# Causal attention stage on one Trainium2 core: rearranging q, k, x, maxima, denominators and outputs through DRAM images

## The chip, the core and the metric

The program runs on one core of a Trainium2 chip. A core has TensorE (PE in the profile; PEld is its weight loads), VectorE (DVE), ScalarE (ACT), GpSimd (POOL) and SyncE (SP), which here issues nearly all DMAs. The metric is the device time of one execution in microseconds (us); before the change the median of three runs is 1862.79 us (1861.15 to 1863.95).

## What is computed

The input is x of 4 batches x 1024 tokens x 256 features, all float32. Two parts follow each other: a causal attention with 16 heads of 16 features, then two layers of local attention and feed-forward. The change lies in the first part alone:

```python
def _L0_attn_ref(x, wq, bq, wk, bk, wv, bv, wo, bo):   # x is layernorm(x)
    q, k, v = proj(wq, bq), proj(wk, bk), proj(wv, bv)      # 16 heads of 16
    scores = jnp.einsum('bhqd,bhkd->bhqk', q, k) * scale
    mask = jnp.triu(jnp.full((t, t), NEG, jnp.float32), k=1)
    attn = jax.nn.softmax(scores + mask, axis=-1)
    out = jnp.einsum('bhqk,bhkd->bhqd', attn, v)
    out = out.transpose(0, 2, 1, 3).reshape(b, t, d)
    return out @ wo + bo

x = x + _L0_attn_ref(_layernorm(x), ...)
x = x + _L0_ffn_ref(_layernorm(x), ...)        # the two local layers
```

## The kernel before

**Chunks.** The causal stage works in 16 chunks n = 0 to 15, each one batch (n div 4) and four heads (n mod 4). A head has 16 features and takes a strip of 32 partitions, so that four heads fill the 128 partitions of a tile and TensorE multiplies the four side by side. `qbuf` and `kbuf` hold q and k of four chunks in turn (chunk n in buffer n mod 4). Row 16 of each strip carries the row maximum in q and -1 in k, so that the product of the turned scores already has the maximum taken off.

**Two passes over the scores.** In chunk n, TensorE makes the scores of chunk n+1 with queries in the partitions ("s", line 928). VectorE reduces them to row maxima (lines 936 and 938, into `nmax`). At the same time TensorE makes the scores of chunk n with keys in the partitions ("t", also line 928), ScalarE takes their exponentials (line 949, `et`), GpSimd zeroes what lies above the diagonal (line 955), and TensorE multiplies by the values (line 985, "av"). The value tile has a column of ones, so that row 16 of each output strip is the softmax's denominator. ScalarE copies each product out of PSUM and GpSimd adds it up (lines 1003 and 1004).

**Slots and the plan.** A chunk has 9 slots (`NU`). A slot u runs `pair(n, u, 0)`, `pair(n, u, 1)` (the s and t products of four heads), the value products of the slot before, and then whatever `plan[n][u]` lists. The plan is written by hand with `put(n, u, function)`, and a u of 9 or more falls into the next chunk. Nothing reorders it: every engine, and SP's queue of DMAs too, runs its instructions in the order in which the code emits them. Score products that need the second half of q (tokens 512 and on), or the maxima of the second half, begin in slot 2, in the second of its two groups.

**The jobs in the plan.**
- `norm`, `prep_x`, `turn_x` (lines 770, 783, 805): layer norm of the next batch, during the first two chunks of a batch (n mod 4 = 0 and 1). `turn_x` turns blocks of 32 x 32 on VectorE and issues 16 DMAs for each group of four token tiles, which put the blocks in their places in `xnT`.
- `project` (864): a quarter of the q or k projection for two chunks, 16 matmuls, into `dense`. `prep_b` (826): the values of two token tiles, 32 matmuls.
- `spread` (883): 16 rows of `dense` into each strip of `qbuf` and `kbuf`, 8 DMAs of 32 KB for one chunk's half.
- `put_maxima` (963), at slots 3 and 8 for the halves 0 and 1 of the next chunk: one turn on VectorE (`mt`), four DMAs to a DRAM tile `way`, and one DMA back into row 16 of the strips of `qbuf` (line 972), which waits for the four.
- `put_out` (1011) and `put_oT` (1022), for half 0 at slots 4 and 5 and for half 1 at slots 1 and 2 of the next chunk: VectorE turns the 128x512 sum (line 1014) and takes the reciprocal of the denominators (1016), GpSimd multiplies (1017), VectorE turns back (1026), and four DMAs move the 16 rows of each head into `oT` (1030).
- `out_b`, `out_s`, `out_c` (1035, 1054, 1068): output projection of two token tiles (32 matmuls), the sum with x, and its layer norm into `y_sb`. They run at slots 7 and 8 of a batch's last chunk and at 5 and 8 of the chunk after it.
- `swap_x` (1064) writes a batch's x to DRAM (`x_keep`) at slot 8 of chunks 6, 10 and 14; `load_x` brings a later batch in; `load_attn`, `load_tab` and `scale_tab` load and scale the weights and tables of the first local layer in chunks 2 to 5.

Of the kernel before, what the change touches and what calls it, by code (L numbers as in the profile page):

```python
# [51 lines left out]
def kernel_body(  # L52
# [621 lines left out]
    with actx:  # L674
        aw = actx.enter_context(tc.tile_pool(name="aw", bufs=1))
        a1 = actx.enter_context(tc.tile_pool(name="a1", bufs=1))
        a2 = actx.enter_context(tc.tile_pool(name="a2", bufs=2))
        a4 = actx.enter_context(tc.tile_pool(name="a4", bufs=4))
        a5 = actx.enter_context(tc.tile_pool(name="a5", bufs=5))
# [37 lines left out]

        nmax = aw.tile([P, 2, STRIP], F32, name="nmax")

        oT = aw.tile([P, 2, T], F32, name="oT")  # L720

        def clear():

            nc.vector.memset(qbuf[1], 0.0)
            nc.vector.memset(kbuf[1], -1.0)
            nc.vector.memset(qbuf[2], 0.0)
            for v in v_sb:
                nc.gpsimd.memset(v[:, :, H * VW :], 0.0)
                nc.gpsimd.memset(
                    v[:, :, 0 : H * VW].rearrange("p k (h s) -> p k h s", s=VW)[  # L730
                        :, :, :, ONE : ONE + 1
                    ],
                    1.0,
                )

        def clear_more():
            nc.gpsimd.memset(kbuf[2], -1.0)
            nc.gpsimd.memset(qbuf[3], 0.0)
            nc.gpsimd.memset(kbuf[3], -1.0)

# [17 lines left out]
        WARM = 26  # L758
        stats, xnTs, dense, avs_, mxs = {}, {}, {}, {}, {}
        qTs, kTs = (lambda n: qbuf[n % 4]), (lambda n: kbuf[n % 4])  # L760
# [43 lines left out]

        def turn_x(b, g, i):

            if i == 0:
                stats[b, "turn"] = b2.tile([P, GRP, 2, 4, 32], F32, tag="xturn", name=f"xturn_{b}_{g}")
            xturn = stats[b, "turn"]
            for t in (2 * i, 2 * i + 1):  # L810
                nc.vector.transpose(
                    xturn[:, t].rearrange("p c j r -> p (c j r)"), stats.pop((b, "xn", GRP * g + t))
                )
            if i == 0:
                return
            dst = xnTs[b][:, GRP * g : GRP * g + GRP].rearrange("p t c n -> p (t c) n")
            src = xturn.rearrange("p t c j r -> p (t c) j r")
            for d in range(4):
                for a in range(4):
                    j = (a + d) % 4  # L820
                    nc.sync.dma_start(  # L821
                        dst[32 * j : 32 * j + 32, :, 32 * a : 32 * a + 32],
                        src[32 * a : 32 * a + 32, :, j, :],
                    )

# [57 lines left out]
        def spread(n, h, kq=nc.sync):  # L883

            b, c = divmod(n, NC4)
            ts = slice(h * 512, (h + 1) * 512)
            for which, dst in enumerate((qTs(n), kTs(n))):
                for j in range(4):
                    r = (c % 2) * 64 + j * HD
                    (kq if which else nc.sync).dma_start(  # L890
                        dst[STRIP * j : STRIP * j + HD, ts],
                        dense[b, c // 2, which][r : r + HD, ts],
                    )

        def pair(n, u, pr):
# [67 lines left out]
        def put_maxima(n, qb):  # L963

            mt = a2.tile([P, STRIP], F32, tag="mt", name=f"mt_{n}_{qb}")
            nc.vector.transpose(mt, nmax[:, qb, :])
            way = keep4.tile([4 * GRP, P], F32, tag="way", name=f"way_{n}_{qb}")
            for a in range(4):
                nc.sync.dma_start(
                    way[:, 32 * a : 32 * a + 32], mt[32 * a : 32 * a + 4 * GRP, :]  # L970
                )
            nc.sync.dma_start(
                qTs(n)[ONE:P:STRIP, qb * 512 : (qb + 1) * 512],
                way.rearrange("(j i) x -> j (i x)", j=4),
            )

        def products(n, u):
# [14 lines left out]
            if kt == 0:  # L992
                avs_[n, "acc"] = a2.tile([P, 512], F32, tag="avs", name=f"avs_{n}_{qb}")
                (nc.vector.tensor_copy if n == NCH - 1 else nc.scalar.copy)(avs_[n, "acc"], av)
# [16 lines left out]
        def put_out(n, qb):  # L1011
# [7 lines left out]
            )  # L1019
            avs_[n, "t1", qb] = t1  # L1020

        def put_oT(n, qb):
# [68 lines left out]
        def quarters(n, b, d, first, *slots):  # L1091
            for i, u in enumerate(slots):
                put(n, u, project, b, d, (first + i) % 2, (first + i) // 2)

        for n in range(NCH):
            b, c = divmod(n, NC4)
            more = b + 1 < B
            if n >= 1:
                put(n, 1, put_out, n - 1, 1)
                put(n, 2, put_oT, n - 1, 1)  # L1100
            put(n, 4, put_out, n, 0)
            put(n, 5, put_oT, n, 0)
            if c == 0:
                if b:
                    quarters(n, b, 1, 3, 0, 1, 3, 4, 6)
                    outs(n, 5, b - 1, 2)
                    put(n, 8, out_b, b - 1, 3)
                    put(n, NU + 6, out_s, b - 1, 3)
                    put(n, NU + 7, out_c, b - 1, 3)
                    put(n, 1, spread, n + 2, 0)  # L1110
                    put(n, 2, spread, n + 3, 0)
                else:
                    quarters(n, b, 1, 2, 0, 1, 2, 3, 4, 6)
                    put(n, 2, spread, n + 2, 0)
                    put(n, 3, spread, n + 3, 0)
                put(n, 7, spread, n + 2, 1)
                put(n, NU, spread, n + 3, 1)
            if c == 0 and more:
                for i, u in enumerate((0, 3, NU, NU + 3)):
                    put(n, u, norm, b + 1, 2 * i, 2 * i + 2)  # L1120
                for i, u in enumerate((4, 5, NU + 2, NU + 5)):
                    put(n, u, prep_x, b + 1, i)
                for i, u in enumerate((7, 8, NU + 7, NU + 8)):
                    put(n, u, turn_x, b + 1, i // 2, i % 2)
                n += 1
                quarters(n, b + 1, 0, 0, 4, 5, 7, 8)
                n += 1
                quarters(n, b + 1, 0, 4, 2, 3, 4, 5)
                for i in range(2):
                    put(n, i, spread, n + 2 + i, 0)  # L1130
                    put(n, 5 + i, spread, n + 2 + i, 1)
                for i in range(4):
                    put(n, (0, 1, 7, 9)[i], prep_b, b + 1, i)
                n += 1
                quarters(n, b + 1, 1, 0, 2, 3, 5)
                n -= 3
            if c == 3:
                outs(n, 7, b, 0)
                outs(n, 8, b, 1)
        n = -1  # L1140
        plan[n][0] = [(spread, (0, 1, nc.scalar)), (spread, (1, 0)), (spread, (1, 1))]
        put(n, 3, bias)
        put(n, 2, load_x, 1, 0, NW)
        for i, u in enumerate((4, 5, 6, 7)):
            put(n, u, prep_b, 0, i)
        put(n, 5, clear_more)
        quarters(n, 0, 1, 0, 7, 8)
        put(n, 7, load_x, 2, 0, NW)

        for n in range(-1, NCH - 1):  # L1150
            for half, u in enumerate((3, 8)):
                plan[n][u].insert(0, (put_maxima, (n + 1, half)))
        for b in range(B - 1):
# [233 lines left out]
```

## Time and profile before

| | us |
|---|---|
| median of three runs (lowest, highest) | 1862.79 (1861.15, 1863.95) |
| the profiled execution's own time | 1867.73 |
| its span, first to last instruction | 1866.0 |
| TensorE busy in the span | 1797.8 (96%) |
| VectorE, ScalarE, GpSimd busy | 1349.4, 1022.9, 1131.4 |
| mean granted TensorE clock | 0.974 |
| first exponential of chunk 0, last of chunk 15 | 57.5, 644.1 |
| the 16 chunks, shortest and longest | 28.8, 45.8 |
| SP's issue of one `spread` DMA, of one `turn_x` DMA | 0.59, 0.61 |

How to read it: busy time is the time in which an engine has an instruction in work. The ends of matmuls are modelled, so a busy TensorE may still be waiting a little. The granted clock is the share of TensorE's full speed that the chip allowed. A timeline row gives start, duration, engine, line, operation, `out<-in`, and in brackets the idle time before it with what ended it. "SPq" is SP's own queue: a row there is the issue of DMAs, not their transfer. In a list of waits, a row says who waited for whom, then the us in total, the number of times and the longest.

### The profile page before, as it was taken

What the parts mean: (1) busy time and instruction counts of PE and PEld (TensorE: products, weight loads), DVE (VectorE), ACT (ScalarE), POOL (GpSimd) and SP (SyncE); (2) the same over time, 40 slices, a digit from 0 to 9 for tenths busy, and PEclk for the clock granted to TensorE, in tenths of its full rate; (3) what the DMA queues carried; (4) which work ended last, traced back from release to release, by engine and by line L of the source; (5) the groups of instructions that cost most, each with busy time, mean ns of one, the idle gap of its engine ahead of it and who ended that gap; (6) DMA issues with size and microseconds to landing.
All of it is one profiled execution on the core that took longest, in us unless ns stands there. A gap on an engine that the chain in (4) does not pass through costs nothing.

```text
span 1866.0 us, 46190 instructions
## 1 busy us (share of the span) xinstructions
PE 1797.8 (96%) x16922; PEld 1055.2 (57%) x16922; DVE 1349.4 (72%) x4115; ACT 1022.9 (55%) x2558; POOL 1131.4 (61%) x1359
## 2 busy tenths in 40 slices
PE   8999998998999979889999999999999999999999
PEld 5444444554454345556656656666566656566576
DVE  5886886896889556667868768768667778678642
ACT  1665765775777635444555465554545555555621
POOL 3463584674475476667666666666667577586611
PEclk7998998998999989899999999999999999999999
DMA  3122111211110120455465565655656556555520
GB/s 109 39 34 80 33 34 37 64 34 36 57 27 15 33 74 7 68 98 98 82 105 88 103 102 90 140 95 96 119 121 121 104 100 117 108 106 111 96 51 23
DMA packets 785248, 142.52 MB, mean 76 GB/s; under 512 B 753552, under 2 KB 776064, under 8 KB 784512
## 3 DMA queue, kind: packets, MB, share of 16 engines
q1 hardware_dynamic: 784704, 139.25, 38.4%
q8 instruction: 135, 2.21, 0.5%
q14 instruction: 89, 0.73, 0.1%
q10 hardware_dynamic: 320, 0.33, 0.1%
HBM read 21.25 MB, written 8.65 MB: 16 GB/s over the span
## 4 chain that ended last, share of the span: by engine, by line
PE 84%; DVE 4%; SPq 4%; DMA 2%; POOL 2%; issue 1%; ACT 1%; DVEq 0%; ACTq 0%; POOLq 0%
PE pag L597 16%; PE pf L621 9%; PE t L928 7%; PE pw L507 6%; PE s L928 6%; PE av L985 6%; PE pq L228 5%; PE pk L228 5%; PE pv L228 5%; PE plo L465 5%; PE ls L386 4%; PE pp L765 3%; SPq L327 2%; SPq L821 2%; PE pr L765 1%
## 5 line engine op out<-in xcount | busy, mean ns | idle before, releaser
L949 ACT ACTIVATE et<-t 128x512 f32<-128x512 f32 x558 | 293.4, 602 | 88.4 <-PE s L928 59.0
L928 PE MATMUL t<-qbuf,kbuf 32*128 32x512 f32 (+1 forms) x1488 | 313.5, 513 | 3.2 <-DMA qbuf<-way 3.0
L597 PE MATMUL pag<-hnT,w 128*128 128x512 f32 x704 | 312.3, 593 | 0.8 <-DVE hnT L581 0.8
L928 PE MATMUL s<-kbuf,qbuf 16*128 16x512 f32 (+3 forms) x1440 | 305.3, 516 | 0.8 <-DVE nmax L938 0.8
L418 ACT ACTIVATE e<-e,lnmx 128x192 f32<-128x192 f32 (+2 forms) x512 | 224.0, 439 | 43.5 <-DVE lnmx L411 43.0
L432 POOL TENSOR_SCALAR e<-e,lrsum 128x192 f32<-128x192 f32 (+2 forms) x504 | 202.3, 422 | 21.1 <-DVE lrsum L429 15.6
L597 PEld LDWEIGHTS pag<-hnT,w 128*128 128x128 f32 x704 | 131.7, 190 | 142.4 <-issue 134.2
L928 PEld LDWEIGHTS t<-qbuf,kbuf 32*128 32x128 f32 x1488 | 149.8, 186 | 99.9 <-ACT et L949 37.1
L267 POOL TENSOR_TENSOR rn<-ss,mhalf 128x16 f32<-128x16 f32 x64 | 188.0, 2938 | 5.3
L1004 POOL TENSOR_TENSOR avs<-avs,part 128x512 f32<-128x512 f32 (+2 forms) x105 | 117.1, 1115 | 108.0 <-ACT part L1003 107.7
L264 POOL TENSOR_TENSOR rot<-rot,m 128x1024 f32<-128x1024 f32 x64 | 151.4, 2365 | 50.8 <-DVE m L245 42.8
L621 PE MATMUL pf<-w,act 128*128 128x256 f32 x768 | 173.1, 379 | 0.0
L938 DVE CUSTOM_DVE_ANT_0 s<-s,mask_c,mx 128x512 f32<-128x512 f32 (+1 forms) x240 | 132.7, 619 | 53.8 <-PE s L928 35.2
L928 PEld LDWEIGHTS s<-kbuf,qbuf 16*128 16x128 f32 x1440 | 146.6, 186 | 39.1 <-DVE nmax L938 11.4
L621 PEld LDWEIGHTS pf<-w,act 128*128 128x128 f32 x768 | 145.8, 190 | 26.6 <-issue 7.2
L611 DVE SCALAR_TENSOR_TENSOR act<-pag,cols_sb,ge 128x512 f32<-128x512 f32 x80 | 59.4, 742 | 139.4 <-ACT ge L610 95.0
L985 PE MATMUL av<-et,v_sb 128*32 128x512 f32 (+3 forms) x1536 | 158.5, 501 | 0.8 <-POOL et L955 0.4
L936 DVE TENSOR_REDUCE mx<-s 128x1 f32<-128x512 f32 (+1 forms) x240 | 133.9, 615 | 14.3 <-PE s L928 14.2
L266 POOL TENSOR_SCALAR ss<-ss 128x16 f32<-128x16 f32 x64 | 16.3, 254 | 197.7 <-DVE ss L261 195.6
L411 DVE CUSTOM_DVE_ANT_0 e<-ls,mask_h 128x192 f32<-128x192 f32 x408 | 116.7, 349 | 20.7 <-PE ls L386 20.7
L955 POOL TENSOR_SCALAR_AFFINE_SELECT et<-et 128x256 f32<-128x256 f32 x256 | 98.1, 407 | 54.9 <-ACT et L949 53.5
L507 PE MATMUL pw<-wlo,loT 128*128 128x256 f32 x512 | 129.0, 396 | 0.7 <-ACT loT L498 0.7
(268 smaller groups left out, 3595.0 us busy)
## 6 DMA issues: line engine op xcount, KB each, us to landing
ring_sb<-turned SPq DMA_DIRECT2D x880, 96.0 KB
qbuf<-dense SPq DMA_DIRECT2D x128, 32.0 KB
x_keep<-x SPq DMA_DIRECT2D x4, 1024.0 KB
xr<-x_keep SPq DMA_DIRECT2D x8, 512.0 KB
out_dram<-y_sb SPq DMA_DIRECT2D x16, 256.0 KB
oT<-t SPq DMA_DIRECT2D x126, 32.0 KB
kbuf<-dense SPq DMA_DIRECT2D x120, 32.0 KB
x<-in_x_dram SPq DMA_DIRECT2D x3, 1024.0 KB
```

Source lines behind the costliest of these rows:

```text
L228: nc.tensor.matmul(pq[i], lhsT=lhs[c], rhs=wt[:, c, i * INNER : (i + 1) * INNER], start=(c == 0), stop=(c == 1),)
L264: nc.gpsimd.tensor_tensor(rot, rot, m3, ALU.add)
L267: nc.gpsimd.tensor_tensor(rn[:, :, 0], ss, mhalf, ALU.pow)
L418: nc.scalar.activation(e[:, i, lo:nk], e[:, i, lo:nk], AF.Exp, bias=nmx[:, h : h + 1], scale=-1.0, accum_out=sums[:, h : h + 1],)
L432: by.tensor_scalar(e[:, i, lo:nk], e[:, i, lo:nk], rsum[:, h : h + 1], 1.0, ALU.mult, ALU.mult)
L507: nc.tensor.matmul(pw[:, 0:D], lhsT=oT[:, c, :], rhs=wt[:, c, :], start=(c == 0), stop=(c == 3))
L597: nc.tensor.matmul(pg[half], lhsT=wt[:, c, ff * P : (ff + 1) * P], rhs=hnT[:, c, :], start=(c == 0), stop=(c == 1),)
L621: nc.tensor.matmul(pf[:, 0:D], lhsT=act[:, f, i * P : (i + 1) * P], rhs=wt[:, f, :], start=(f == 0), stop=(f == NF - 1),)
L928: nc.tensor.matmul(o, lhsT=lhsT, rhs=rhs, start=True, stop=True)
L936: nc.vector.tensor_reduce(mxs[n + 1, i][:, h : h + 1], src, AX.X, ALU.max)
L949: nc.scalar.activation(et[:, h % 2, :], ts[h], AF.Exp, scale=ASCALE)
L985: nc.tensor.matmul(av[32 * j : 32 * j + 32, c0:512], lhsT=v_sb[b % 2][:, kt, VW * (4 * c + j) : VW * (4 * c + j) + STRIP], rhs=ets[j // 2] ...
```

## The change

- **DRAM images for q and k.** `img` holds two pairs of DRAM tiles of 256 x 1024, one for q and one for k, already in strips of 32 rows. `put_dense` writes a half of `dense` (128 rows) into the 16 used rows of eight strips, with one DMA each for q and k; `fetch` reads the 128 rows of one chunk's half with one DMA each. The unused rows are filled once by 16 DMAs (`clear_images`). `spread` is left for chunks 0 and 1.
- **Turned x.** `turn_x` writes its blocks to a DRAM tile with one DMA for each two token tiles; `fetch_x` reads a group of four back with four DMAs in rows of 32 values (128 bytes).
- **Maxima.** `put_maxima` writes the whole turned tile with one DMA; `get_maxima`, a slot later, reads it into row 16.
- **Outputs of chunks 0 to 13.** VectorE turns nothing. The denominator rows go out to DRAM (`den_out`), come in as 128 x 16 (`den_in`), VectorE takes the reciprocal and they go out again (`rec_out`), come back spread over each strip's 32 partitions with four DMAs (`rec_in`), and GpSimd multiplies 128x512 by 128x512 (`divide`). The product is written to DRAM, and for each two chunks one DMA (`get_oT`) gathers a half into `oT`. Chunks 14 and 15 keep `put_out` and `put_oT`.
- **The plan.** Projections of the next batch go to slots 4, 5, 6, 8 of the third chunk and 3, 5, 7 of the fourth (they stood at 2, 3, 4, 5 and 2, 3, 5). `out_b` moves from the last two slots of a batch and slots 5 and 8 of the next chunk to slots 5 and 7 of the next chunk and 1 and 2 of the one after, with `out_s` and `out_c` behind each.

The core of the diff:

```diff
+        img = [[keep.tile([2 * P, T], F32, name=f"img{i}{which}") for which in range(2)] for i in range(2)]
+        def clear_images(i):
+            for which, src in enumerate((qbuf[3], kbuf[3])):
+                dst = img[i][which].rearrange("(k r) (x t) -> k r x t", r=STRIP, t=256)
+                for x in range(4):
+                    nc.sync.dma_start(dst[:, HD:STRIP, x], src[:, 0:256])
...
+            nc.sync.dma_start(
+                stats[b, "way"][:, o : o + 4], xturn.rearrange("p t c j r -> p (t c) j r")
+            )
+        def fetch_x(b, g):
-            for d in range(4):
-                for a in range(4):
-                    j = (a + d) % 4
-                    nc.sync.dma_start(
-                        dst[32 * j : 32 * j + 32, :, 32 * a : 32 * a + 32],
-                        src[32 * a : 32 * a + 32, :, j, :],
-                    )
+            for j in range(4):
+                nc.sync.dma_start(
+                    dst[32 * j : 32 * j + 32].rearrange("q k (a r) -> q k a r", a=4),
+                    way[:, :, j, :].rearrange("(a q) k r -> q k a r", a=4),
+                )
...
+        def put_dense(b, d, h):
+                rows_ = img[(NC4 // 2 * b + d) % 2][which].rearrange("(k r) t -> k r t", r=STRIP)
+                nc.sync.dma_start(rows_[:, 0:HD, ts], dense[b, d, which][:, ts])
+        def fetch(n, h):
+            for which, dst in enumerate((qTs(n), kTs(n))):
+                nc.sync.dma_start(dst[:, ts], img[(n // 2) % 2][which][c * P : (c + 1) * P, ts])
...
+        def rec_out(n, qb):
+            nc.vector.reciprocal(rec, avs_.pop((n, "d1", qb)))
+            way = keep4.tile([4, 512], F32, tag="recway", name=f"recway_{n}_{qb}")
+            nc.sync.dma_start(way.rearrange("j (k x) -> (j k) x", x=16), rec)
...
+        def divide(n, qb):
+            nc.gpsimd.tensor_tensor(
+                t3, avs_.pop((n, "out", qb)), avs_.pop((n, "t1", qb)), ALU.mult
+            )
...
+                put(n, 0, get_maxima, n, 1)
+                    for u, fn in ((1, den_out), (2, den_in), (3, rec_out), (4, rec_in), (6, divide)):
+                        put(n, u, fn, n - 1, 1)
+                put(n, 4, get_maxima, n + 1, 0)
+                for u, fn in ((5, den_out), (6, den_in), (7, rec_out), (8, rec_in), (NU + 1, divide)):
+                    put(n, u, fn, n, 0)
...
-                quarters(n, b + 1, 0, 4, 2, 3, 4, 5)
+                quarters(n, b + 1, 0, 4, 4, 5, 6, 8)
+                put(n, 0, put_dense, b + 1, 0, 0)
+                put(n, 3, fetch, n + 2, 0)
+                put(n, 4, fetch, n + 3, 0)
+                put(n, NU, put_dense, b + 1, 0, 1)
+                put(n, NU + 1, fetch, n + 2, 1)
+                put(n, NU + 2, fetch, n + 3, 1)
...
+                    for i, u in enumerate((NU + 5, NU + 7, 2 * NU + 1, 2 * NU + 2)):
+                        outs(n, u, b, i)
```

## The prediction

> **What bounds the kernel now.** I read the page first. TensorE (PE) is busy 96% of the span, so time can only be won where PE stands idle, runs at a lower clock, or is fed too slowly. The change touches only the causal stage, whose last exponential ends at 644 us.
>
> ```profile
> PE 1797.8 (96%) x16922; PEld 1055.2 (57%) x16922; DVE 1349.4 (72%) x4115; ACT 1022.9 (55%) x2558; POOL 1131.4 (61%) x1359
> ```
>
> Second, a table of windows, one for each of the stage's 16 chunks (cut where the first exponential of a chunk, L949, starts). Columns: length, then busy time of PE, PEld, DVE, ACT and POOL, then the granted PE clock, DMA share, GB/s. Chunks 5, 6, 7 and 13:
>
> ```profile
> 247.90:284.10 36.20, 35.57 (x356) 17.38 (x352) 32.65 (x107) 25.30 (x50) 29.27 (x37) 1.00 0.18 31
> 284.10:329.90 45.80, 40.03 (x452) 18.72 (x448) 28.38 (x88) 26.79 (x56) 18.95 (x30) 0.89 0.22 41
> 329.90:365.90 36.00, 35.98 (x436) 18.28 (x435) 29.29 (x94) 26.36 (x53) 19.16 (x29) 1.00 0.21 71
> 555.40:585.50 30.10, 30.10 (x292) 15.11 (x290) 28.95 (x93) 23.28 (x45) 17.45 (x26) 1.00 0.09 20
> ```
>
> Chunk 6 takes 45.8 us where its neighbours take 36, with PE idle for 5.8 and the clock at 0.89; chunks 2 and 10 (45.2, 44.7) look the same. Third, PE's waits, then for chunk 2 SP's timeline, then two short windows, name the cause:
>
> ```profile
> PE pp L765 <- DMA xnT<-xturn: 10.3, 2, 5.7
> PE t L928 <- DMA qbuf<-way: 3.0, 4, 1.6
> ```
> ```profile
> 129.71 11.35 SPq L821 DMA_DIRECT2D xnT<-xturn  x16
> 141.16 2.46 SPq L890 DMA_DIRECT2D qbuf<-dense  x4
> ```
> ```profile
> 141.80:151.80 10.00, 9.03 (x60) 3.41 (x64) 3.04 (x9) 3.45 (x7) 0.73 (x1) 0.50 0.25 52
> 182.80:186.00 3.20, 3.20 (x32) 1.45 (x27) 2.52 (x9) 1.62 (x4) 2.31 (x5) 0.50 0.37 129
> ```
>
> SP needs 11.4 us merely to issue 16 transfers of turned x. PE waits 4.5 us for the last of them (5.75 in chunk 6, 4.4 in chunk 10) and then runs 10 us at clock 0.50. In chunk 3 a wait of 1.57 us for the maxima (L972) ends at 181.06, and some 3.4 us at 0.50 follow. SP's issuing, and the clock that a wait costs, are the prize. The second limit is VectorE: 29.0 of 30.1 us in chunk 13.
>
> **Prices.** PE's work in a chunk without project, prep_b and out_b: chunk 7 is 36.0 less three projections (0.87 each, the spacing of the four at 10.5 to 13.1 us), one prep_b and two out_b (1.9 each, the row of 32 matmuls at 362.83), 27.7; chunk 12 is 35.9 less five and two, 27.8. I use 27.9. A wait with its clock: chunks 2, 6, 10 should take 27.9 + 4 x 0.87 + 3 x 1.9 = 37.1, and chunk 2 takes 8.1 more for a wait of 4.5, so I put 8.5 on a wait of 4.5 us; chunk 3 takes 38.9 - 36.0 = 2.9 more for 1.57, so 3.5 for 2 us, 5 for 3. Waits of 0.6 us (chunk 11) cost no clock.
>
> **What goes.**
> - Turned x takes 2 + 4 transfers a group instead of 16, and its first user moves from slot 2 to slot 4: chunks 2, 6, 10 go from 135.7 to 3 x 37.1, -24.4.
> - VectorE loses two turns of 0.70 us for each half of chunks 0 to 13, 2.8 us a chunk, and the waits of up to 3 us that the second turn has for the transfers before it:
>
> ```profile
> DVE t L1026 <- DMA oT<-t: 5.5, 2, 3.0
> ```
>
> - Chunks 1, 5, 9 hold four projections only (27.9 + 3.5 = 31.4 us of PE) but take 36.9, 36.2 and 35.8, with VectorE busy 32: here its relief is worth time. And two out_b a batch move from chunks 3, 7, 11 to 5, 9, 13. With no new wait: chunk 1 31.4 (-5.5); 5 and 9 35.2 (-1.6 together); 3, 7, 11 32.4 (-14.1); 13 31.7 (+1.6); 4, 8, 12 36.05 (-1.2); 14 -0.7.
>
> Together **-46**; if VectorE is not what stretches chunks 1, 5 and 9, about -31. Cost nothing: the memsets taken from VectorE and GpSimd, and the 16 image-clearing issues (8 us of SP) beside chunks -1 and 0; get_maxima behind the first eight has four slots of cover.
>
> **What comes: SP's queue ahead of slot 2.** The maxima of half 1 are turned by VectorE (mt) just as a chunk begins. Slot 2 of that chunk needs them, and half 1 of the next chunk's q, 7.3 us later (chunk 7: mt at 329.74, second group of slot 2 at 337.02). Today they land after 5.4:
>
> ```profile
> 330.32 1.91 SPq L969 DMA_DIRECT2D way<-mt  x4
> 333.35 0.54 SPq L972 DMA_DIRECT2D qbuf<-way  x1
> 334.00 0.37 SPq L1066 DMA_DIRECT2D x_keep<-x  x1
> ```
>
> In the new order get_maxima stands behind all that slot 8 plans, and small transfers also wait for the bytes issued before them: in chunk 3 the four 2 KB writes behind the 1.5 MB weight load landed 5.2 us after the last issue, not 1.1 as here. I walk the queue from mt with 0.5 us an issue (L969 takes 0.46, large loads 0.35 to 0.58), 1.1 us to the first byte, and for 256 KB in 2 KB rows 0.8 us (the weights, 320 GB/s) to 1.5 us (the tables' 1 KB rows, 172 GB/s).
> - Chunks 7, 11: maxima out, get_oT, four rec_in, **x_keep (1 MB, 3.1 us at 320 GB/s), which now stands ahead**, two put_dense, get_maxima, then fetch, which waits until put_dense has landed. q lands 11.0 to 12.9 us after mt: a wait of 3.7 to 5.6. I take 4.5, 8.5 with its clock: +17. Chunk 3, without x_keep, waits 0.6 to 2.5, taken as 2: +3.5.
> - Chunk 1: four rec_in, four reads of turned x (4096 pieces of 128 B; the old transfers show 32.6% of 16 queues x 11.1 us over 4352 packets, 13.3 ns each, so 3.4 us), two fetches, get_maxima: landed at about 9.3, wait 2, +3.5. Chunks 5 and 9 now have an out_b ahead of slot 2: wait 1 each, +2. Chunks 2, 6, 10 have two prep_b there: 0.5 each, +1.5.
> - Chunk 15 reaches slot 2's second group 4.8 us after mt; x_keep and four output issues now stand in front: wait 3, +5.
>
> **GpSimd.** The divide is 128x512, 1.27 us (the row of L1004) for 0.62 (L1017), +18 us in all, but its 61 us of waiting for the reciprocal go, and two slots lie between rec_in and divide. What costs is the move of two out_b: their adds and out_c now meet prep_x and scale_tab (2.4 each) in chunk 5, where POOL is busy 29.3 already. The masks of slots 1 and 2, which the value products need, come 2 to 4 us late: +3. VectorE's reciprocal waits for den_in, issued one slot before; behind it stand the score evictions, and so PE. The path (POOL's sum, two landings of 2 us) leaves some 1.5 us: nothing, but about 1 us a chunk if that cover is gone.
>
> New costs: 17 + 3.5 + 3.5 + 2 + 1.5 + 5 + 3 = 35.5 (12 at the lower ends without clock, 55 at the upper with it). **Net -11**: the span of 1866.0 becomes 1855. The profiled run took 1867.7, the median is 1862.8; the same 11 off the median is **1852**.
>
> **Two rules that bear on it.** Half clock after 1.57 us of idling stands in the trace. The Trainium skill ("TensorE: Matmul & The Clock Gate", Part 1) has the clock fall only after a whole idle window of about 3.4 us; by it the waits of 2 and 3 us would cost no clock, and the sum would be an estimated 5 us better. No transfer here has an outermost count of eight. The skill ("DMA: Bandwidth & Descriptors", on why a DMA increments its semaphore by 16) spreads a DMA over the largest number up to 16 that divides the outermost counts of both sides, so put_dense and get_oT would get 8 of the 16 engines; by an estimate from that page, the sum would be 6 us worse.
>
> **Rivals.**
> - *Forecast, 45%*: **1852**, between 1838 and 1866.
> - *The queue hides it, 22%*: transfers run at 320 GB/s, waits stay under a microsecond outside chunks 7, 11 and 15, new costs 12: -34, **1829**. For it: chunk 7 has 1.9 us of cover today. Against: x_keep's new place.
> - *Slower, 25%*: the small reads. Turned x is now read from DRAM in pieces of 128 B, which no row shows. At 20 ns a piece instead of 13.3 the four reads take 1.7 us longer, directly ahead of q and the maxima in chunks 1, 2, 5, 6, 9, 10; waits of 2 to 4 us with their clock then cost 4 more each, +24: **1876**. From about 16 ns on the 11 us are used up.
> - *It doesn't do what it says, 8%*: x of the second group still lands after slot 4, and chunks 2, 6, 10 keep most of their wait: 1863.
>
> **Numbers.** 0.2%, 3.7 us, is about what a measurement of this kernel can tell from no change. Of the forecast's 45, 36 are faster, 5 the same, 4 slower; the second case is faster, the third slower, the fourth the same: faster 0.58, same 0.13, slower 0.29. The range takes in the second and third case with a little around them: 1826 to 1878.
>
> **What would show it.** Right: chunks 2, 6, 10 near 37 us with no wait for xnT; PE waits on qbuf<-way or qbuf<-img at slot 2 of chunks 7, 11, 15 with clock 0.50 after each; POOL over 33 us in chunk 5. Wrong: chunks 1, 5, 9 still at 36 with VectorE below 30 (then something else paced them); slot 2 without waits; or VectorE waiting for its reciprocals in every chunk.

## The result, and the profile after

The changed kernel is slower: 1878.4 us median of 4 runs (1877.4 to 1879.7) where the kernel before took 1863.4 in the same session (1861.2 to 1864.3). The ratio is 1.0083, with a 95% interval of 1.0065 to 1.0100. The forecast was 1852.

| profiled execution | before | after |
|---|---|---|
| its own time, span (us) | 1867.7, 1866.0 | 1878.5, 1876.7 |
| causal stage, first to last exponential | 57.5 to 644.1 | 54.6 to 669.1 |
| everything behind it | 1221.9 | 1207.6 |
| PE idle in the stage; periods at clock 0.50 there | 20.0; 4, 34 us in all | 32.0; 10, 71 us in all |

The stage became 28 us longer. It began 2.9 us sooner (so it did in a second profile of the kernel before), and the part behind it, whose code is the same, became 14.3 us shorter: the span shows only 10.7 of the 28.

The page of after. The instruction counts fell on VectorE (4115 to 4058), but PE, with the same 16922 matmuls, is busy longer:

```profile
span 1876.7 us, 45891 instructions
PE 1801.9 (96%) x16922; PEld 1056.2 (56%) x16922; DVE 1323.3 (71%) x4058; ACT 1023.1 (55%) x2558; POOL 1146.9 (61%) x1358
```

The table of windows of after, chunks 5, 6, 7 and 13, with the columns of the prediction:

```profile
245.40:290.80 45.40, 44.02 (x424) 22.72 (x426) 40.87 (x118) 27.06 (x51) 41.79 (x50) 0.92 0.37 95
290.80:333.50 42.70, 39.13 (x452) 19.23 (x451) 25.85 (x85) 26.75 (x56) 20.12 (x29) 0.92 0.33 84
333.50:372.60 39.10, 35.55 (x368) 16.70 (x362) 24.61 (x80) 25.14 (x51) 16.68 (x27) 0.91 0.40 131
570.20:605.90 35.70, 35.30 (x358) 17.95 (x355) 30.43 (x100) 24.44 (x48) 30.35 (x42) 1.00 0.27 84
```

Chunk 6 was to fall from 45.8 to 37 and stands at 42.7, with its clock still at 0.92. Chunk 5, which had run at 36.2 with its clock at 1.00, takes 45.4: GpSimd (the last busy time) went from 29.3 to 41.8 of it, VectorE from 32.7 to 40.9.

What PE waited for in the stage, and one wait of VectorE (us in all, times, longest). Waits for xnT are gone. Those for the maxima grew from 3.0 to 26.1:

```profile
DVE rec L1066 <- DMA d<-den: 26.6, 17, 3.1
PE t L953 <- DMA qbuf<-way: 26.1, 8, 4.7
...
PE s L953 <- DVE nmax L963: 3.1, 3, 1.4
...
PE s L953 <- DMA qbuf<-img: 1.8, 3, 0.8
```

SP's timeline at the start of chunk 2 (start, length, instruction) says why:

```profile
127.16 0.32 SPq L993 DMA_DIRECT2D way<-mt  x1
127.57 2.79 SPq L832 DMA_DIRECT2D xnT<-xway  x4
130.47 3.32 SPq L1076 DMA_DIRECT2D t<-recway  x4
133.89 1.39 SPq L911 DMA_DIRECT2D img<-dense  x2
135.32 0.56 SPq L999 DMA_DIRECT2D qbuf<-way  x1
```

The maxima leave at 127.2, and only 8.2 us later SP comes to the instruction that reads them back (L999). Four reads of turned x, four of reciprocals and two image writes stand between them. Of the 3.32 us at L1076 some 1.5 are waiting, as the same four take 1.80 where nothing is waited for (chunk 7). L999 itself then needs 4 us, behind 512 KB of image writes: the chain of waits, in chunk 6, has the 8 KB as one piece of 4.25 us:

```profile
298.27 0.63 SPq L911
298.90 0.04 issue
298.94 4.25 DMA qbuf<-way
```

The stage by groups of chunks, in us. "Forecast" is the prediction's sum with its costs (the 3 us for GpSimd put to chunks 5 and 9); it adds to 576, the measured chunks to 614.5.

| chunks | 1 | 2, 6, 10 | 3, 7, 11 | 4, 8, 12 | 5, 9 | 13 | 15 | all 16 |
|---|---|---|---|---|---|---|---|---|
| before | 37.0 | 135.8 | 111.3 | 109.3 | 72.0 | 30.1 | 28.8 | 586.5 |
| forecast | 34.9 | 112.8 | 117.7 | 108.2 | 75.4 | 31.7 | 33.8 | 576.0 |
| after | 40.8 | 126.5 | 120.4 | 107.3 | 88.2 | 35.6 | 33.6 | 614.5 |

Two places hold most of the miss of 38.5: chunks 2, 6, 10 (13.7) and chunks 5, 9, 13 (16.7). So the first theory (Q) was that SP's order at the chunk boundaries makes the loss, through late maxima; the second (B or P) that it is the output path, by the places of its projections or by its own transfers.

### The profile page after: what moved, and what is told of

It is laid out like the page before. It is cut to its first block, busy times and chain, and to the rows that moved or that the text cites. A ratio compares the mean times of both kernels' runs of the same rounds, so it can differ in the third digit from the quotient of the medians.

```text
span 1876.7 us, 45891 instructions
## 1 busy us (share of the span) xinstructions
PE 1801.9 (96%) x16922; PEld 1056.2 (56%) x16922; DVE 1323.3 (71%) x4058; ACT 1023.1 (55%) x2558; POOL 1146.9 (61%) x1358
## 3 DMA queue, kind: packets, MB, share of 16 engines
q1 hardware_dynamic: 810608, 174.79, 43.6%
## 4 chain that ended last, share of the span: by engine, by line
PE 83%; SPq 4%; DMA 4%; DVE 4%; POOL 2%; issue 1%; ACT 1%; ACTq 0%; DVEq 0%; POOLq 0%
PE pag L597 15%; PE pf L621 8%; PE t L953 8%; PE av L1014 7%; PE pw L507 6%; PE s L953 6%; PE pq L228 5%; PE pk L228 5%; PE pv L228 5%; PE plo L465 4%; SPq L327 3%; PE ls L386 3%; PE pp L773 3%; PE pr L773 1%; DMA qbuf<-way 1%
## 5 line engine op out<-in xcount | busy, mean ns | idle before, releaser
L953 PE MATMUL t<-qbuf,kbuf 32*128 32x512 f32 (+1 forms) x1488 | 326.3, 530 | 26.3 <-DMA qbuf<-way 26.1
L953 PE MATMUL s<-kbuf,qbuf 16*128 16x512 f32 (+3 forms) x1440 | 316.1, 535 | 5.0 <-DVE nmax L963 3.1
L953 PEld LDWEIGHTS t<-qbuf,kbuf 32*128 32x128 f32 x1488 | 158.4, 197 | 118.9 <-ACT et L974 33.8
L264 POOL TENSOR_TENSOR rot<-rot,m 128x1024 f32<-128x1024 f32 x64 | 151.4, 2366 | 44.6 <-DVE m L245 36.7
L953 PEld LDWEIGHTS s<-kbuf,qbuf 16*128 16x128 f32 x1440 | 151.2, 197 | 47.9 <-DVE nmax L963 13.9
L621 PE MATMUL pf<-w,act 128*128 128x256 f32 x768 | 173.1, 379 | 0.0
L1014 PE MATMUL av<-et,v_sb 128*32 128x512 f32 (+3 forms) x1536 | 165.0, 521 | 0.4
L621 PEld LDWEIGHTS pf<-w,act 128*128 128x128 f32 x768 | 145.8, 190 | 26.6 <-issue 7.2
L963 DVE CUSTOM_DVE_ANT_0 s<-s,mask_c,mx 128x512 f32<-128x512 f32 (+1 forms) x240 | 132.5, 619 | 39.6 <-PE s L953 37.4
L963 DVE CUSTOM_DVE_ANT_0 s<-s,mask_c 128x384 f32<-128x384 f32 (+2 forms) x240 | 110.3, 522 | 61.5 <-PE s L953 58.4
```

Of the source, the lines that this page charges most:

```text
L264: nc.gpsimd.tensor_tensor(rot, rot, m3, ALU.add)
L621: nc.tensor.matmul(pf[:, 0:D], lhsT=act[:, f, i * P : (i + 1) * P], rhs=wt[:, f, :], start=(f == 0), stop=(f == NF - 1),)
L953: nc.tensor.matmul(o, lhsT=lhsT, rhs=rhs, start=True, stop=True)
L963: nc.vector.tensor_tensor_reduce(out=src, in0=src, in1=mask_c[:, 512 - w : 512], scale=1.0, scalar=mxs[n + 1, i][:, h : h + 1] if k0 else ...
L1014: nc.tensor.matmul(av[32 * j : 32 * j + 32, c0:512], lhsT=v_sb[b % 2][:, kt, VW * (4 * c + j) : VW * (4 * c + j) + STRIP], rhs=ets[j // 2] ...
```

## The experiments

Ratios are to the kernel before, from runs on the same chip. At 1863 us, 0.001 is 1.9 us. The table gives each run's chunks; the sections tell what they were for. Single executions of one kernel differ by up to 0.9%, so a difference of a few us is read from the chunks of the profile, not from the median.

| run | ratio, 95% | 1 | 2, 6, 10 | 3, 7, 11 | 5, 9 | 13 | 15 | all 16 |
|---|---|---|---|---|---|---|---|---|
| after | 1.0083, 1.0065 to 1.0100 | 40.8 | 126.5 | 120.4 | 88.2 | 35.6 | 33.6 | 614.5 |
| maxima first | 1.0039, 1.0018 to 1.0059 | 42.6 | 107.8 | 124.3 | 92.7 | 36.7 | 29.5 | 603.2 |
| outs later | 1.0125, 1.0084 to 1.0165 | 40.0 | 126.3 | 120.8 | 91.6 | 38.6 | 33.5 | 626.6 |
| x_keep later | 1.0017, 1.0000 to 1.0035 | 40.7 | 124.5 | 116.2 | 91.1 | 35.6 | 31.8 | 610.0 |
| old outputs, old places | 0.9827, 0.9795 to 0.9860 | 37.9 | 109.7 | 113.9 | 73.3 | 30.1 | 29.9 | 567.1 |
| old outputs, new places | 0.9876, 0.9830 to 0.9921 | 37.1 | 109.9 | 105.0 | 89.5 | 33.8 | 29.7 | 572.4 |
| reciprocals off the boundary | 0.9968, 0.9951 to 0.9985 | 39.7 | 110.1 | 114.4 | 88.7 | 34.4 | 33.5 | 591.9 |
| turned x alone | 0.9894, 0.9864 to 0.9924 | 35.1 | 108.8 | 114.3 | 78.4 | 30.1 | 29.9 | 568.9 |
| old outputs, add on GpSimd | 0.9862, 0.9832 to 0.9892 | 38.1 | 109.7 | 117.0 | 73.1 | 29.9 | 29.9 | 570.6 |
| old outputs, SP order | 0.9788, 0.9766 to 0.9809 | 35.1 | 109.0 | 109.4 | 75.0 | 30.1 | 28.6 | 559.6 |
| change, SP order | 0.9872, 0.9848 to 0.9895 | 35.6 | 108.1 | 105.6 | 90.5 | 36.0 | 31.9 | 576.8 |
| change, SP order, GpSimd relieved | 0.9788, 0.9763 to 0.9814 | 36.3 | 109.7 | 102.1 | 74.7 | 32.3 | 33.3 | 559.8 |

**Maxima first.**

```
-                put(n, 0, get_maxima, n, 1)
...
                 put(n, u, put_maxima, n + 1, half)
+                if half and n >= 0:
+                    put(n, u, get_maxima, n + 1, 1)
```

> The reading back of half 1's maxima (L999) is issued directly behind their writing out (L993) at the end of a chunk, ahead of the reads of reciprocals, of turned x and of the images; nothing else moves. Theory Q (SP's order sets the loss): the waits of PE for qbuf<-way in chunks 1, 2, 3, 6, 7, 10, 11 and 15, 26 us in all, and the periods at clock 0.50 behind them, 58 us, go; chunks 1, 2, 6, 10 come to 37 to 38 us, chunks 3, 7, 11 keep 1 to 2 us of wait for the image of q; the time falls by 25 to 45 us, to 1833 to 1853. Theory E (the load of VectorE and GpSimd sets it): the waits go but their time is given back by waits for VectorE, and the time falls by less than 8 us, to above 1870.

It gained 8 us by the ratio, far less than theory Q had given. The median, 1872.7, is where theory E had put it, but not for E's reason: the time was not given back by waits for VectorE. Chunks 2, 6 and 10 came to 35.9 us each at clock 1.00. But the wait of chunks 1, 3, 7 and 11 moved to the image of q, whose write and reading back now stand behind SP's stop for the maxima to land. PE's waits in the stage of this run:

```profile
PE s L953 <- DMA qbuf<-img: 27.1, 6, 7.8
PE s L953 <- DVE nmax L963: 3.4, 4, 1.4
PE t L953 <- DMA qbuf<-way: 1.0, 1, 1.0
```

Maxima and images cost 27.9 us together in the changed kernel and 28.1 here. Slot 2 needs both, and one of them stands behind the rest. Theory Q holds in a stricter form: SP's backlog at the boundary is too long, and who stands first in it only says which chunks pay.

**Outs later.**

```
-  for i, u in enumerate((NU + 5, NU + 7, 2 * NU + 1, 2 * NU + 2)):
+  for i, u in enumerate((NU + 5, NU + 7, 2 * NU + 4, 2 * NU + 6)):
```

> The output projections of the second half (out_b with out_s and out_c) move from slots 1 and 2 to slots 4 and 6 of the second chunk of a batch; the rest is as in the changed kernel. Theory B (in chunks 5, 9, 13 GpSimd and VectorE are overfull at the start of the chunk only): slots 0 and 1 of chunks 5, 9, 13 fall by 2 to 4 us each and the time falls by 10 to 20 us, to 1858 to 1868. Rival (two more projections in these chunks are too much wherever they stand): slots 4 to 8 take up what slots 0 to 2 give, and the time changes by less than 3 us.

Slower by 8 us, though the intervals of the two ratios overlap, and the stage by 12: neither theory came. Slots 0 and 1 of chunk 5 took 7.2 and 7.8 us, where they had taken 7.9 and 7.3, so the two projections moved away were not what fills them. What still stands there on GpSimd are the out_c of the first pair, prep_x, scale_tab and the division. The moved ones lengthened slots 4 and 6 (5.5 and 2.9 to 5.9 and 4.7; in chunk 9 4.9 and 2.9 to 6.6 and 4.7), and their out_c came into slot 0 of chunk 6 (4.7 to 6.4).

**x_keep later.**

```
-  put(NC4 * (b + 1) + 2, 8, swap_x, b)
+  put(NC4 * (b + 1) + 3, 3, swap_x, b)
   if b + 3 < B:
-      put(NC4 * (b + 1) + 3, 1, load_x, b + 3, 0, NW)
+      put(NC4 * (b + 1) + 3, 4, load_x, b + 3, 0, NW)
```

> The write of x_keep (1 MB) moves from the last slot of chunks 6, 10, 14 to slot 3 of chunks 7, 11, 15, the load of x behind it to slot 4. Theory Q with the prediction's price (the write holds up the small transfers behind it by 3.1 us): the waits for qbuf<-way in chunks 7, 11, 15 (3.0, 4.3, 3.8 us) fall to the 1.3 us of chunk 3, and the time falls by 9 to 14 us, to 1864 to 1869. Rival (the issues and the half-used writes of images make the wait, the 1 MB runs beside them): each of these waits falls by less than 1 us and the time by less than 4 us.

The waits for the maxima in chunks 7, 11 and 15 fell from 3.0, 4.3 and 3.8 us to 1.0, 1.6 and 2.0, as theory Q had it. The median fell by about 12 us, but the profiled execution (the longest of ten) shows 4.9 us less in chunks 7, 11 and 15, so 12 is not well supported. Of the prediction's 17 us for chunks 7 and 11 the write's own share is 3.1 (80.9 to 77.8).

**Old outputs, in old and in new places.** Two runs part the output path from the places of its projections. In the first all chunks take put_out and put_oT, with the output projections where the kernel before had them. In the second they stay in the places of the change; there the projections read rows of oT that the next batch has partly overwritten, which changes values and no instruction.

```
         def old_out(n):
-            return n >= NCH - 2
+            return True
...
-                put(n, 7 if n < NCH - 1 else 4, put_out, n, 0)
-                put(n, 8 if n < NCH - 1 else 5, put_oT, n, 0)
+                put(n, 4, put_out, n, 0)
+                put(n, 5, put_oT, n, 0)
```

The first run alone also has

```
+                outs(n, 7, b, 0)
+                outs(n, 8, b, 1)
+                if more:
+                    outs(n, NU + 5, b, 2)
+                    put(n, NU + 8, out_b, b, 3)
```

> The output path of the kernel before (turned twice on VectorE, four transfers) for all chunks, with its output projections in the places they had before; turned x, images of q and k and maxima as in the changed kernel. Theory Q: SP loses up to 3.3 us of issuing ahead of L999 in every chunk, so the waits for qbuf<-way in chunks 1, 2, 6, 10 fall to under 1 us, those of chunks 7 and 11 by about 2 us; chunks 5, 9, 13 come back to 36, 36 and 30 us; the time falls by 25 to 40 us, to 1838 to 1853. Rival (the pieces of 128 B of turned x and the writes of the images make the waits): chunks 5, 9 and 13 come back, but the waits stay above 2 us, and the time falls by 10 to 18 us.

> The output path of the kernel before for all chunks, as in the run above that had it, but the output projections stay in the places of the change (slots 5 and 7 of a batch's first chunk, 1 and 2 of its second). It parts the two halves of that run's gain of some 45 us on the changed kernel. Theory P (the path through DRAM images, its transfers on SP and its work on GpSimd, makes the loss): chunks 5, 9, 13 take 37 to 40 us (33 for chunk 13), and the time is 1833 to 1845. Theory B (the places make it): chunks 5, 9 and 13 stay at 42 us and more, and the time is above 1850.

The first run, at 1835 us beyond what theory Q had given, is 1.7% faster than before and 2.6% faster than the change: the other three parts of the change together are a gain, and the outputs, path and places, spoil it. The second gives up 9 us of it (0.0049). So the path costs the larger part, 0.0207 or 39 us, and the places 9. Their share is not where theory P had put it, though: chunks 5 and 9 stay at 47.6 and 41.9 us in the new places, as theory B said; other chunks get most of that back (3, 7, 11 take 8.9 us less, 4, 8, 12 4.8). The path's cost lies in the chunks that waited for the maxima: 1, 2, 3, 6, 7, 10, 11 and 15 hold 39.6 of the 42.1 us by which the stage of the second run is shorter than that of the change. With four reads of reciprocals fewer at the boundary, PE's waits in the first run are

```profile
PE t L953 <- DMA qbuf<-way: 5.8, 6, 1.7
...
PE s L953 <- DMA qbuf<-img: 2.0, 2, 1.0
```

**Reciprocals off the boundary.** All of the change stays; only the reads of a first half's reciprocals leave the last slot of the chunk.

```
-  ((5, den_out), (6, den_in), (7, rec_out), (8, rec_in), (NU + 1, divide))
+  ((5, den_out), (6, den_in), (7, rec_out), (NU + 2, rec_in), (NU + 3, divide))
```

> The changed kernel with the four reads of reciprocals of a chunk's first half (L1076) moved from the last slot of the chunk to slot 2 of the next, behind the reading of the maxima; the division follows one slot later, get_oT one slot later, the first two output projections one slot later, and t1 has two buffers. Theory Q2 (these reads, with SP's wait for the reciprocals to land, are what makes L999 late): the waits for qbuf<-way in chunks 1, 2, 6, 10 fall from 2.7 to 4.7 us to under 1.5, and with their clock the chunks come to 36 to 39 us; the time falls by 15 to 30 us, to 1848 to 1863. Rival (turned x and the image writes are enough to hold SP up): the waits fall by less than 1 us each and the time by less than 8 us.

21 us faster than the change, inside what theory Q2 gave. Chunks 2, 6, 10 took 36.0, 37.2 and 36.9. At the start of chunk 2, L999 now comes 4.7 us after the maxima, where it had come after 8.2:

```profile
126.48 0.32 SPq L993 DMA_DIRECT2D way<-mt  x1
126.89 2.79 SPq L832 DMA_DIRECT2D xnT<-xway  x4
129.78 1.31 SPq L911 DMA_DIRECT2D img<-dense  x2
131.20 0.63 SPq L999 DMA_DIRECT2D qbuf<-way  x1
```

Chunk 1 kept its 4.5 us of wait: it was not these reads alone there.

**Turned x alone**, on the kernel before (turn_x, fetch_x and their slots, with the slots of norm and prep_x that come with them; nothing else):

> The kernel before with the turned x through a DRAM image alone (turn_x, fetch_x and the slots of norm, prep_x and turn_x as in the change); q, k, maxima and outputs as before, projections in their old slots. By the prediction's sum chunks 2, 6 and 10 fall from 45 to 37 us each: 24 us faster than before, 1835 to 1845. Rival (VectorE's and SP's other work holds these chunks, or the pieces of 128 B make the maxima late): at most 10 us faster, above 1853.

20 us faster, the chunks as forecast: 36.1, 36.5 and 36.1 for 45.2, 45.8 and 44.7, with no wait for xnT, though the projections that use it keep their old slots here. The first term of the prediction's sum was right in mechanism and size. It is not free elsewhere: chunks 5 and 9 took 6.4 us longer than before (78.4 for 72.0). In chunk 5 PE waited 1.89 us for a mask of GpSimd, and 13.7 us at clock 0.50 went with it. Fewer issues and earlier slots were not tried apart.

**The addition on GpSimd.** In the changed kernel's chunk 5 one small instruction of VectorE takes 6.05 us. VectorE's timeline, and below it GpSimd's (start, length):

```profile
257.75 6.05 DVE L160 TENSOR_SCALAR ve_a<-mv 128x2 f32<-128x2 f32 x1
263.71 0.42 DVE L963 CUSTOM_DVE_ANT_0 s<-s,mask_c 128x256 f32<-128x256 f32 x1
```
```profile
257.48 2.36 POOL L119 TENSOR_TENSOR tab<-tab,sc 128x1024 f32<-128x1024 f32 x1
259.79 1.48 POOL L980 TENSOR_SCALAR_AFFINE_SELECT et<-et 128x256 f32<-128x256 f32 x4
261.24 1.27 POOL L1132 TENSOR_TENSOR x<-x,add 128x512 f32<-128x512 f32 x1
262.47 1.30 POOL L1084 TENSOR_TENSOR t<-avs,t 128x512 f32<-128x512 f32 x1
263.88 0.72 POOL L162 TENSOR_TENSOR rs_a<-ve_a,mhalf 128x2 f32<-128x2 f32 x1
```

It starts while GpSimd works and ends when GpSimd first pauses, seven instructions later; the next one, L162, needs its result. At its shortest this addition takes 0.17 (the median in norm); four others of the 24 in this stage took 1.05 to 1.45.

```
-        nc.vector.tensor_scalar_add(ve[:, 0:n], var, EPS)
+        nc.gpsimd.tensor_scalar_add(ve[:, 0:n], var, EPS)
```

> The run with the old output path, with one instruction more moved: the addition of epsilon to 128x2 variances (L160 in norm and out_s) runs on GpSimd, next to the power that follows there, and not on VectorE. In the traces that addition takes 0.17 us on VectorE when GpSimd is idle and up to 6.05 us when GpSimd runs instruction behind instruction. Theory L (VectorE is shut out until GpSimd pauses, and the scores behind it make PE wait): the long ones of chunks 5 and 9 (1.1, 3.1, 2.3 us in that run) go and the time falls by 2 to 6 us against that run, to 1826 to 1831. Rival (PE has other work meanwhile): the same within 2 us, or slower by the 0.7 us that each costs GpSimd.

No gain: the ratio is 0.0035 higher than in the run it changes, and the two intervals overlap. VectorE's stalls went, chunk 9 gained 1.8, but chunks 5, 7 and 11 lost 1.6, 1.1 and 2.0. The stall is real; that it costs PE time could not be shown.

**Old outputs, SP order,** and **the change, SP order.** Three moves: maxima are read back as the first thing of a chunk, except in the last chunk of a batch, where the image's write goes first; turned x is read one slot later; x_keep is written at slot 3. One run makes them on the run with the old outputs, one on the run with the reciprocals off the boundary, which has every part of the change.

```
+        for n in range(1, NCH):
+            if n % NC4 != 3:
+                put(n, 0, get_maxima, n, 1)
...
-                put(n, 8, fetch_x, b + 1, 0)
-                put(n, NU + 8, fetch_x, b + 1, 1)
+                put(n, NU, fetch_x, b + 1, 0)
+                put(n, 2 * NU, fetch_x, b + 1, 1)
```

> The run with the old output path and places, with SP's order mended at the chunk boundaries: maxima are read back (L999) as the first thing of a chunk, except in the last chunk of a batch, where the images' writes go first; turned x is read (L832) one slot later, behind the maxima and the image of q; x_keep is written at slot 3 instead of the slot before the boundary. What is left of waits for qbuf<-way and qbuf<-img in that run is 1.7 us in chunk 1, 0.9 in 5, 1.5 and 1.7 in 7 and 11, 1.6 in 15, with 10 us at clock 0.50. Theory Q (SP's order): most of it goes, 6 to 12 us faster than that run, ratio to the kernel before 0.976 to 0.980. Rival (landing times, not order, make what is left, or VectorE's 35 us in chunks 1, 5 and 9 do): within 3 us of that run, ratio 0.981 to 0.985.

> The changed kernel with all of its parts, its output path and its places, and three moves in SP's order: the reads of reciprocals of a first half off the chunk boundary (as in the run that had only this), maxima read back first except in the last chunk of a batch, turned x one slot later, x_keep at slot 3. Theory Q: the waits at slot 2 of chunks 1, 5, 9 (4.5, 3.4, 3.1 us with only the first move), 7 and 11 (2.4, 3.3) and 15 (4.0) fall to under 1.5 us each; 12 to 25 us faster than with the first move alone, 1835 to 1850, though chunks 5 and 9 stay at 40 us or more for their two output projections. Rival (SP has too many issues in these chunks, so the waits move to the images): less than 6 us faster than with the first move alone.

Both times came as theory Q gave them: 0.0039 (7 us) and 0.0096 (18 us) off the run each started from. The intervals of the first pair just overlap; its stage became 7.5 us shorter. At the start of chunk 2 of the second, L999 is issued 1.4 us after the maxima leave:

```profile
121.79 0.32 SPq L993 DMA_DIRECT2D way<-mt  x1
123.20 0.56 SPq L999 DMA_DIRECT2D qbuf<-way  x1
123.86 3.35 SPq L832 DMA_DIRECT2D xnT<-xway  x4
```

PE's waits for maxima and images fell to 6.2 us in all, from 27.9 in the changed kernel and 26.1 with the reciprocals off the boundary. Two of over 1.5 us are left, 2.29 in chunk 3 and 2.18 in chunk 15. Chunks 5 and 9 stay at 47.3 and 43.1.

**GpSimd relieved.** On top of the last run, the out_c of a batch go to its third chunk, where GpSimd is busy for 20 of 36 us, and the two scale_tab from chunk 5 to 7.

```
-                        outs(n, u, b, i)
+                        put(n, u, out_b, b, i)
+                        put(n, u + 1, out_s, b, i)
+                        put(n, 3 * NU + 1 + 2 * i, out_c, b, i)
...
-        put(5, 0, scale_tab, 0, 0)
-        put(5, 1, scale_tab, 0, 1)
+        put(7, 1, scale_tab, 0, 0)
+        put(7, 3, scale_tab, 0, 1)
```

> The run with all parts of the change and SP's order mended, with GpSimd relieved in the chunks that are a batch's second: the four out_c of a batch (two instructions of 1.22 us each) move to slots 1, 3, 5, 7 of its third chunk, and the two scale_tab (2.35 us each) from chunk 5 to chunk 7; their small tiles get four buffers. In the run before, chunks 5, 9 and 13 take 47, 43 and 36 us with GpSimd busy 42, 37 and 30, where PE's own work, four projections and two output projections, is 35. Theory G (GpSimd, full at the start of these chunks, holds the masks that PE's value products need, and holds VectorE off): they fall to 36 to 39 us (13 to 33) and the time falls by 10 to 18 us, ratio to the kernel before 0.977 to 0.982. Rival V (VectorE's norm, out_s and score work, or the half clock behind its waits, makes them long): they stay at 41 us or more, the time falls by less than 5 us.

As theory G gave it: 0.0084, 16 us, off that run, and chunks 5, 9 and 13 took 37.8, 36.9 and 32.3 us. First the window of chunk 5 in the run it changes, then those of chunks 5, 6, 7 and 13 of this run:

```profile
229.20:276.50 47.30, 44.32 (x421) 21.78 (x420) 38.39 (x116) 26.63 (x51) 41.69 (x47) 0.89 0.34 90
```
```profile
230.50:268.30 37.80, 37.78 (x422) 19.73 (x422) 33.74 (x117) 26.37 (x51) 27.46 (x37) 1.00 0.41 114
268.30:305.30 37.00, 36.57 (x453) 18.36 (x452) 25.85 (x84) 26.39 (x55) 28.14 (x35) 1.00 0.37 97
305.30:338.80 33.50, 32.89 (x372) 15.76 (x366) 24.44 (x80) 25.17 (x51) 22.70 (x31) 1.00 0.50 153
518.20:550.50 32.30, 32.27 (x353) 16.17 (x346) 27.86 (x97) 24.06 (x47) 20.58 (x31) 1.00 0.29 88
```

GpSimd does the same work, 10 to 14 us a batch of it in another chunk, and the clock is 1.00 in all four. Which half of theory G counts was not parted: PE's waits for masks in chunk 5 went (3.0 us), and VectorE's longest addition of this kind fell from 4.18 to 1.21 us. Two kernels so beat both: this one, with every part of the change, and the old outputs with SP's order, both 2.1% faster than before (0.9788).

**The kernel before, again.**

> The kernel before, once more, as a control of what a profile of the same kernel varies by. Theory: the causal stage ends within 2 us of 644.1 us, chunks 2, 6, 10 at 45 us; the part behind it is 1222 us within 3 us, so that the 14 us by which that part is shorter in the changed kernel belong to the change. Rival: the part behind the stage varies by 10 us between executions of the same kernel, and the 14 us are chance.

The stage ended at 644.7 us, chunks 2, 6, 10 took 45.0, 43.8 and 45.6, and the part behind the stage 1219.1. So the 14.3 us by which that part is shorter after the change are more than this one repetition's difference of 2.8. All runs with images of q and k show 1207 to 1215 there, turned x alone 1218. Some 5 of the 14.3 are idle time of PE: 42.5 us of it behind the stage in before and 43.6 in the repetition, but 37.1 in after and 35.1 to 39.5 in the other runs with images. The rest goes with periods at clock 0.50, 43.6 us in all behind the stage in before and 26.5 in after; in the other runs of this record they come to 29.8 to 41.0, so that share may be chance. In before the waits that are longer than in after are PE's for ring_sb 170 to 230 us behind the stage, and one some 730 us behind it for which the profile names no cause. Why the images should shorten either stays open.

## Why the prediction was wrong

- **Turned x (-24.4): right.** Chunks 2, 6, 10 without other waits take 108 to 110 us together (111.3 forecast); the wait for xnT is gone.
- **VectorE's relief in chunk 1 (-5.5), 5 and 9 (-1.6): too much.** With hardly a wait left chunk 1 takes 35.1 to 36.3, not 31.4, whether VectorE is relieved or not: 35.1 with the old outputs and SP's order, where VectorE is busy 31.5, and 35.6 with the change and SP's order, where it is busy 29.1. In the change's places chunks 5 and 9 took 74.7 at best, not 70.4. The prediction had the sign for it ("still at 36 with VectorE below 30"). The base of 27.9 for PE's work, taken from chunks 7 and 12, looks too low as well: chunk 14, which holds none of the extra work, took 29.7 before and 29.6 in after, with VectorE a microsecond less busy. With that base chunk 1 would come to 33; what paces it at 35 is not shown.
- **Chunks 2, 6, 10, wait 0.5 each (+1.5): the step that failed.** Only the two prep_b were held against the queue, and the queue itself was not walked for these chunks, as it was for 1 and 7. In chunk 2 it stood 8.2 us long at L999, and PE went on 12.4 us after the maxima left. The waits were 2.8, 3.6 and 2.7, not 0.5, and with the clock the three chunks took 18 us more than with SP's order mended (126.5 against 108.1). Moving the path's four reads, with SP's stop for the reciprocals before them, gave 16 of it back (110.1), with the reads of turned x and the image writes still in front of L999 and waits of at most 0.7 us.
- **GpSimd (+3) and the waits of 5 and 9 (+2): the second step that failed.** Out_c was named as a meeting with prep_x and scale_tab, but priced as a delay of masks. In the pair of runs that differ in this, chunks 5, 9, 13 fell from 126.5 to 107.0 us, so its price there was 19.5, and 16 in the whole. The sign named for it came (POOL over 33 us in chunk 5: 41.8), its size not. GpSimd was busy for 33.1 of the first 33.9 us of chunk 5 in after; the average of the chunk before, 29 of 36 us, hid how little room there was.
- **Chunks 7, 11 (+17), 3 (+3.5), 1 (+3.5), 15 (+5): together near.** Forecast 29; these chunks took 194.8 us in after and 173.1 with SP's order mended, 22 less, with 2.2 us of wait still in chunk 15. The single sizes were off and partly made up for each other. In chunks 3, 7, 11 the waits were smaller than forecast (1.3, 3.0, 4.3, and for the maxima where the walk had the image of q land last), in chunk 1 larger (4.7, not 2).
- **The reciprocal wait (nothing): it exists, 26.6 us in all.** By the prediction's own sign ("VectorE waiting for its reciprocals in every chunk") the forecast was in doubt. But it cannot have cost much: in the last kernel, with GpSimd relieved, 22.7 us of it remain, and the stage takes 559.8 us, as long as the old outputs with SP's order (559.6), which have no such wait in these chunks.
- **The rival of small reads: its number came by luck.** It gave 1876, close to the measured 1878.4, but its cause was wrong: a piece of 128 B took a median of 13.0 ns, close to the prediction's 13.3, not 20. The four reads hold SP for 2.8 us of issuing and so were a part of the queue in front of the maxima.
- **The part behind the stage (no term): -14.3 us.** Without it the miss would have been larger.
- **Small slips:** 1 MB at 320 GB/s takes 3.3 us, not 3.1; and the small writes of chunk 3 landed 4.8 us after the last issue, if measured as the 1.1 of chunk 7 is, not 5.2. Neither moves the sum by a microsecond.

**The two rules.** In chunk 5 of after a wait of 1.35 us is followed by 6.8 us at clock 0.50 (PE's row, then a window with the columns as above):

```profile
250.94 0.61 PE L953 MATMUL s<-kbuf,qbuf 16*128 16x384 f32 x1 [1.35 <-DVE nmax L963]
```
```profile
251.40:258.20 6.80, 6.80 (x50) 4.14 (x50) 6.11 (x27) 2.76 (x5) 6.80 (x7) 0.50 0.96 172
```

A wait of 2.29 us in chunk 3 of the change with SP's order is followed by none. The rule that the prediction cites from the Trainium skill ("TensorE: Matmul & The Clock Gate", Part 1: a whole idle window of about 3.4 us) does not fit the first, and the trace decides; the prediction's fixed price for a wait does not fit the second. During the image writes of chunk 2 the DMA engines were busy for 0.49 of their time, with next to nothing else running, and for 0.99 during the reading of an image (columns as above, the last two are DMA share and GB/s):

```profile
136.20:138.90 2.70, 0.62 (x8) 0.22 (x8) 0.00 (x0) 0.65 (x2) 1.79 (x2) 0.97 0.49 174
96.00:98.10 2.10, 0.00 (x0) 0.00 (x0) 0.24 (x1) 0.00 (x0) 0.93 (x2) 0.92 0.99 316
```

That agrees with the rule on the outermost count in the Trainium skill ("DMA: Bandwidth & Descriptors", on why a DMA increments its semaphore by 16), by which the write gets 8 of the 16 engines. The prediction had left it out of its sum, and the 4.25 us that the 8 KB of maxima take behind such writes is part of what was missed.

## What to carry to other kernels

In an in-order queue, walk the whole queue for every place where a wait can end, not only for the place that looks worst; and count the transfers that wait inside it, since each holds up what stands behind it. Fewer transfers in one path do not help if another path, put beside it, adds its own where an urgent one must pass. When work is moved to an engine with room on average, look at the slots it lands in: here moving the same GpSimd work one or two chunks on took 19.5 us off chunks 5, 9 and 13 and put 2.8 on chunks 6, 10 and 14.

## What the runs showed of the hardware

- An addition on 128x2 elements on VectorE took 6.05 us while GpSimd ran seven instructions without a pause, and 0.17 us at its shortest. The Trainium skill ("SBUF — State Buffer", Who interferes with whom) has the loser of a shared port wait for the whole instruction of the other; here it waited for a row of seven. Not every overlap does it: at 272.48 us of after an addition of the same size took 0.17 beside an out_c.
- Periods at clock 0.50 in the stage lasted 3.4, 6.8, 10.2 or (outs later, turned x alone) 13.7 us. PE's waits next to them were from 0.5 us (old outputs in new places, chunk 5) to 7.9 us (maxima first, chunk 11).
- Reading 8 KB rows to write x_keep ran at 414 GB/s, 2 KB rows of an image at 316, pieces of 128 B at 155 (windows of after around 338, 97 and 130 us).
